# Layer 0 of a two-layer graph network with experts: aggregating normalized tokens and multiplying by the weights afterwards

## The chip, the cores and the metric

The kernel runs on one core of a Trainium2 chip. The metric is the device time of one execution in microseconds (us); several executions are measured and the median counts. The engines are TensorE (PE, with its weight loads shown apart as PEld), VectorE (DVE), ScalarE (ACT), GpSimd (POOL) and SyncE (SP), which here only issues DMAs.

## The reference

3327 tokens of 256 features go through two layers. Each layer is a graph aggregation followed by a mixture of 8 experts of which every token uses 2. Cut to what matters here (layer 0; layer 1 has another aggregation and other experts and isn't touched):

```python
def _L0_gnn_ref(x, adj, W, b):
    support = jnp.matmul(x, W)              # 256x256 weights
    out = jnp.matmul(adj, support) + b      # adj: 3327x3327
    return jax.nn.relu(out)

x = x + _L0_gnn_ref(_layernorm(x), adj, L0_gnn_W, L0_gnn_b)
x = x + _L0_ffn_ref(_layernorm(x)[None], Wg, bg, W1, b1, W2, b2)[0]   # top 2 of 8 experts
x = x + _L1_gnn_ref(_layernorm(x), adj, ...)
x = x + _L1_ffn_ref(_layernorm(x)[None], ...)[0]
```

So layer 0 computes adj · (LN(x) · W) + b. All of it is in float32.

## The kernel before, in words

**Tiles.** The tokens are padded to 3328, which is 26 tiles of 128 (`NT`). `x` [128, 26, 256] holds the tokens and stays in SBUF, and `s` of the same shape holds what the aggregation reads. The transposed adjacency matrix is read in 13 panels of 256 output tokens (`PW`, `NPAN`). A panel is two pieces of 13 tiles each (`NCHUNK`, `CJ`), 1664 KB a piece. Six pieces fit into a ring of buffers (`ring`, `RING`), which is three panels; `load_panel` (L335) loads them on SP's queue.

**Feature stage (L1022 to L1039).** For groups of 2, 2, 4, 4, 6 and 8 tiles DVE computes mean and 1/deviation (`statistics`, L258). PE turns each tile of `x` with transposes (`turned_tiles`, L304), ACT copies the result to SBUF (L305), PE multiplies it by `proj_sb` (`node_features`, L312), and ACT scales it by 1/deviation into `s` (L317). The mean is taken out of the weights once, with two matmuls (L1030) and one subtraction on DVE (L1033). So PE has 52 transposes and 52 products of [128x128] by [128x256] here, and the trace shows each float32 product as two instructions.

**Aggregation (`aggregate`, L344).** For each panel PE takes the pieces as weights and `s` as the moving operand, 52 products (L358), and gets the sums token by token in two PSUM tiles `ps_g`. DVE adds bias, ReLU and `x` (`add_relu`, L322, L323). ACT counts for each panel how many elements of the adjacency matrix are positive (`count`, L1046: 8 `sign` instructions a piece), which layer 1 needs.

**After a panel (`after0`, L1056).** DVE normalizes the panel's tokens (`layernorm`), multiplies them by the gate's weights (`scores`, L378, 16 instructions), takes the two best experts (`top_two`, `rt_both` L415) and their softmax (`weights`; the exponential is on ACT, L443). A panel later `list_tokens` (L457) ranks the tokens of each expert with small matmuls on PE (`pr`, L464 and L465), and POOL scatters the rows to the experts' lists in DRAM (`scatter`, L482). The engines work in the order in which the program's scheduler put the instructions, and each engine's queue is in order.

**Zeros of the lists (`fill`, L1003).** The first 256 rows of each expert's list, of both layers, are set to zeros with a spare row number in column `ID` (the last of 258). For each of the 16 lists POOL sets a [128, 2 x 258] tile (L1009, L1010) from a pool of two, and SP writes it to DRAM in rows of 1032 bytes (L1013). This is in `after0` of panels 0 and 1. `after0` of panel 0 also turns the two gates' weights by two DMAs from DRAM to DRAM of 2048 elements of 4 bytes each (L1062), and POOL loads the first to all partitions (`load_gate`, L247).

**After the panels.** The experts' blocks start at L865 on PE. Their first two steps don't need the last panel's tokens.

**DMA on SP.** SP's DMAs share eight completion semaphores in turn, so a DMA is issued only when the eighth before it has landed.

Of the kernel before, what the change touches and what calls it, by code (L numbers as in the profile page):

```python
# [22 lines left out]
P = 128  # L23
# [53 lines left out]

BEGUN, FIRST_TILES, MORE_TILES = 12, 14, 22
WARM = 32
# [11 lines left out]
def gnn_moe_two_layers(  # L91
# [39 lines left out]

    proj_sb = const.tile([P, DC, D], F32, name="proj_sb")
    for t, n in [(0, 2)] + [(t, 4) for t in range(2, NT, 4)]:
        nc.sync.dma_start(out=x[:, t : t + n, :], in_=x_in[:, t : t + n, :])
        if t == 0:
            nc.sync.dma_start(out=proj_sb, in_=g0_w.rearrange("(c p) n -> p c n", p=P))
# [10 lines left out]
    mean = ring[RING - 1][:, 0:P]  # L147
    nc.gpsimd.memset(mean, 1.0 / D)
# [95 lines left out]
    gates = []  # L244

# [62 lines left out]
    def node_features(i, lhsT, w_sb, scale=None):  # L308
# [6 lines left out]
        if scale is None:  # L315
            return nc.scalar.copy(s[:, i, :], ps)
        return nc.scalar.activation(s[:, i, :], ps, AF.Copy, scale=scale)  # L317
# [12 lines left out]
    def piece(pan, k):  # L330
        return ring[(pan * NCHUNK + k) % RING].rearrange("p (c w) -> p c w", w=PW)

    last_piece, output_loads = [], []

    def load_panel(pan, prepare, earlier=()):  # L335

        for k in range(NCHUNK):
            a = piece(pan, k)
            with behind(earlier):
                d = nc.sync.dma_start(out=a, in_=adjT[pan, k])  # L340
            last_piece[:] = [d]
            prepare(pan, k, a)

    def aggregate(b_sb, prepare, after, loaded=0, count=None):  # L344

        for pan in range(NPAN):
# [4 lines left out]
            if count:  # L351
                count(pan, chunks)
# [14 lines left out]
            after(pan)  # L367

# [634 lines left out]
    def fill(xlist):  # L1003

        with tc.issue_after(last_feature.ins):
            for e in range(E):
                zeros = blk.tile([P, H // P, SB], F32, name="wide").rearrange("p h b -> p (h b)")
                zeros = zeros[:, 0 : SG * RW].rearrange("p (g d) -> p g d", g=SG)
                nc.gpsimd.memset(zeros, 0.0)  # L1009
                nc.gpsimd.tensor_scalar(  # L1010
                    zeros[:, :, ID], slot, float(AWAY + SPARE + (LATE + e) * SB), None, ALU.add
                )
                nc.sync.dma_start(  # L1013
                    out=xlist[e * NP : e * NP + SB, :].rearrange("(g p) d -> p g d", p=P),
                    in_=zeros,
                )

    deviation = {}
    for t0, n0 in [(0, 2), (2, 2), (4, 4), (8, 4), (12, 6), (18, 8)]:  # L1022
        _, rs = statistics(t0, n0)
        deviation.update((t0 + g, rs[:, g : g + 1]) for g in range(n0))
        for t in range(t0, t0 + n0, 2):
            xT = turned_tiles([x[:, t + g, :] for g in range(2)])
            if t == 0:
                ps = psy.tile([P, D], F32, name="ps_mean", tag="py")
                for c in range(DC):
                    nc.tensor.matmul(  # L1030
                        ps, lhsT=mean, rhs=proj_sb[:, c, :], start=(c == 0), stop=(c == DC - 1)
                    )
                nc.vector.tensor_tensor(  # L1033
                    proj_sb, proj_sb, ps.unsqueeze(1).to_broadcast([P, DC, D]), ALU.subtract
                )
            for g in range(2):
                last_feature = node_features(
                    t + g, xT[:, :, ts(g, P)], proj_sb, deviation[t + g]
                )  # L1039

    def count(pan, chunks):
        with tc.issue_after(last_feature.ins):
# [451 lines left out]
```

## Time and profile before

| | |
|---|---|
| median of 3 executions | 1244.86 us (1243.46 to 1245.89) |
| the profiled execution | 1245.38 us, its span 1243.6 us, 1.8 us around it |
| PE busy | 1202.0 us, 97% of the span |
| first aggregation matmul of layer 0 | starts at 44.30 us |
| last aggregation matmul of layer 0 | ends just before 344.87 us |
| layer 0's panels, first to last | 300.6 us for 13 |

The span runs from the first instruction to the last. A row of a timeline has its start and its duration in us, the engine ("SPq" is SP's queue), the line, the instruction and the tiles as out<-in. A row of waits names who waited for whom: total us, times, longest. A row by stage has for each engine the busy time and the instructions, then PEclk (the granted TensorE clock as a share of full speed), the DMA engines' busy share and GB/s.

### The profile page before, as it was taken

Reading aid. Unit: us, or ns where it says so; the run is one execution under the profiler, and the core shown is the slowest. Engines: PE = TensorE matmul, PEld = TensorE weight load, DVE = VectorE, ACT = ScalarE, POOL = GpSimd, SP = SyncE. Lnnn points to the kernel's source line nnn. Section 1 sums busy time; section 2 is a strip of 40 time slices with the busy share of each in tenths; the row PEclk is TensorE's granted clock in tenths of the full one; section 3 lists DMA queues with packets and bytes.
Section 4 is the critical chain, followed back from the end, with each engine's and each line's share of the span. In section 5 each row is a group of like instructions: output and inputs, shape, how many; then the busy total and the mean of one; then the engine's idle time right before and its main releaser. Section 6 shows DMA issues by size and latency. Waiting matters only on the chain. (4 is left out here: it accounts for less than half of the span.)

```text
span 1243.6 us, 18251 instructions
## 1 busy us (share of the span) xinstructions
PE 1202.0 (97%) x5853; PEld 1040.3 (84%) x5853; DVE 698.0 (56%) x2812; ACT 522.5 (42%) x963; POOL 280.9 (23%) x367
## 2 busy tenths in 40 slices
PE   7999899999999999999999999999999999999993
PEld 6888788888888888888888888888888888877882
DVE  5064967768755111211111166658999998875464
ACT  4785654551022222222232235895555453043331
POOL 2022313112122111111111110002422323254441
PEclk9999899999999999999999999999999999999997
DMA  9568445544266567575757676344554442476697
GB/s 346 169 194 279 158 169 200 179 146 155 98 215 208 181 197 237 178 230 180 232 173 242 209 273 237 110 149 152 192 182 167 166 176 85 122 247 206 200 296 236
DMA packets 119738, 241.60 MB, mean 194 GB/s; under 512 B 21568, under 2 KB 90192, under 8 KB 112592
## 3 DMA queue, kind: packets, MB, share of 16 engines
q1 hardware_dynamic: 107984, 208.23, 50.2%
q0 software_dynamic: 11104, 31.59, 7.0%
q8 instruction: 48, 0.79, 0.3%
q14 instruction: 58, 0.48, 0.1%
q10 hardware_dynamic: 544, 0.52, 0.1%
HBM read 203.99 MB, written 36.33 MB: 193 GB/s over the span
## 5 line engine op out<-in xcount | busy, mean ns | idle before, releaser
L358 PE MATMUL ps_g<-s,ring 128*128 128x256 f32 x2704 | 591.0, 381 | 0.0
L358 PEld LDWEIGHTS ps_g<-s,ring 128*128 128x128 f32 x2704 | 514.2, 191 | 69.2
L865 PE MATMUL ps_h<-xT,ring 128*128 128x256 f32 (+1 forms) x1176 | 250.1, 366 | 2.7 <-DVE xT L856 1.1
L865 PEld LDWEIGHTS ps_h<-xT,ring 128*128 128x128 f32 x1176 | 205.5, 191 | 39.2 <-ACT wide L872 4.8
L872 ACT ACTIVATE wide<-ps_h,ring 128x256 f32<-128x256 f32 (+1 forms) x240 | 110.2, 459 | 286.0 <-PE ps_h L865 285.0
L378 DVE SCALAR_TENSOR_TENSOR rt_product<-xn,gate 128x256 f32<-128x256 f32 x400 | 197.0, 493 | 12.4
L904 PE MATMUL ps_y<-ring,wide 128*128 128x256 f32 x896 | 200.4, 379 | 0.0
L482 POOL DMA_INDIRECT xlist<-xn,rt_idx x104 | 106.3, 1023 | 371.6 <-DVE ln_ve L269 296.0
L904 PEld LDWEIGHTS ps_y<-ring,wide 128*128 128x128 f32 x896 | 167.2, 190 | 20.9
L1046 ACT ACTIVATE sign<-ring,below 128x416 bf16<-128x416 f32 x208 | 133.5, 642 | 71.6 <-DMA ring<-in_adjT 65.5
L482 POOL DMA_INDIRECT ys<-narrow,index x56 | 54.3, 969 | 331.9 <-DVE narrow L912 245.9
L1197 ACT ACTIVATE ring<-ring 128x3328 f32<-128x3328 f32 x22 | 65.4, 2979 | 87.2 <-DVE ring L1196 56.6
L856 DVE COPY xT<-ptb 128x512 f32<-128x512 f32 (+1 forms) x29 | 19.0, 654 | 146.3 <-PE ptb L853 146.3
L911 DVE TENSOR_TENSOR narrow<-ps_y,ring 128x256 f32<-128x256 f32 x56 | 23.8, 424 | 133.7 <-PE ps_y L904 132.2
L322 DVE TENSOR_TENSOR gnn_t<-ps_g,gnn_b_sb 128x256 f32<-128x256 f32 x52 | 21.9, 421 | 119.4 <-PE ps_g L358 106.4
L482 POOL DMA_INDIRECT ys<-wide,index x58 | 57.8, 996 | 61.2 <-DVE wide L912 35.3
L1198 ACT ACTIVATE ring<-ring 128x3328 f32<-128x3328 f32 x22 | 65.4, 2979 | 0.6
L872 ACT ACTIVATE narrow<-ps_h,ring 128x256 f32<-128x256 f32 (+1 forms) x64 | 28.9, 453 | 68.6 <-PE ps_h L865 66.5
L443 ACT ACTIVATE rt_d<-rt_d 128x2 f32<-128x2 f32 x26 | 5.3, 202 | 123.2 <-DVE rt_d L442 123.2
L904 PE MATMUL ps_y<-s,narrow 128*128 128x256 f32 (+1 forms) x200 | 49.0, 386 | 0.1
L266 DVE BATCH_NORM_STATS2 ln_st<-x 128x6 f32<-128x256 f32 x104 | 42.9, 419 | 6.1 <-DMA x<-in_x 5.0
L1196 DVE TENSOR_SCALAR ring<-ring 128x3328 f32<-128x3328 f32 x22 | 41.3, 1882 | 0.0
(212 smaller groups left out, 983.9 us busy)
## 6 DMA issues: line engine op xcount, KB each, us to landing
ring<-in_adjT SPq DMA_DIRECT2D x52, 1664.0 KB, 7.3
ring<-in_f_w1T SPq DMA_DIRECT2D x30, 1024.0 KB, 6.1
ring<-in_f_w2T SPq DMA_DIRECT2D x30, 1024.0 KB, 7.8
ring<-xlist SPq DMA_DIRECT2D x52, 258.0 KB, 3.0
ring<-in_f_w SPq DMA_DIRECT2D x36, 256.0 KB, 3.6
ring<-ys SPq DMA_DIRECT2D x14, 512.0 KB, 5.2
ring<-in_f_b SPq DMA_DIRECT2D x34, 128.0 KB, 8.0
xlist<-wide SPq DMA_DIRECT2D x16, 258.0 KB, 6.4
```

The costliest lines, as they stand in the source:

```text
L266: nc.vector.bn_stats(out=st, in_=x[:, t0 + g, :])
L358: nc.tensor.matmul(ps[it], lhsT=chunks[k][:, c, ts(it, P)], rhs=s[:, j, :], start=(j == 0), stop=(j == NT - 1),)
L378: nc.vector.scalar_tensor_tensor(product, xn[:, g, 0, 0:D], 1.0, gate[:, e, :], ALU.mult, ALU.mult, accum_out=sc[:, g, e : e + 1],)
L482: d = nc.gpsimd.indirect_dma_start(out=a[:, :], out_offset=bass.IndirectOffsetOnAxis(ap=index, axis=0), in_=rows_, in_offset=None,)
L865: nc.tensor.matmul(ps, lhsT=w1[:, c, ts(hc, P)], rhs=xT[:, c, :], start=(c == 0), stop=(c == DC - 1),)
L872: nc.scalar.activation(hT[:, hc, :], ps, func, bias=bb1[:, hc : hc + 1])
L904: last_product[:] = [nc.tensor.matmul(ps, lhsT=hT[:, hc, ts(g, P)], rhs=w2[:, hc, :], start=(hc == 0), stop=(hc == hc_n - 1),)]
L911: nc.vector.tensor_tensor(y[:, g, :], ps, bb2, ALU.add)
L1046: nc.scalar.activation(sign, a[:, :, ts(i, GROUP)], AF.Sign, bias=below, accum_out=positive[:, pan, i, k : k + 1],)
L1196: nc.vector.tensor_scalar(a, a, 0.0, None, ALU.max)
L1197: nc.scalar.activation(a, a, AF.Square)
L1198: nc.scalar.activation(a, a, AF.Tanh)
```

## The change

1. The feature stage is gone. DVE normalizes each tile straight into `s` (`layernorm(..., xn=s[...])`, one instruction a tile more), with the same groups and the same statistics.
2. The aggregation is `aggregate_first`. `s` gives the weights and the panel's piece is the moving operand, so the sums come out turned: two PSUM tiles [128 features x 256 tokens]. The number of products is the same, 52 a panel. ACT copies the two sums to SBUF (`g`), and PE multiplies them by `proj_sb`, 4 products a panel (`finish`), 6 tiles (`BEHIND` = 5) into the next panel, or at once after the last one. `add_relu` and `after0` of the panel follow `finish`.
3. Panels 0 and 1 go side by side over the first 13 tiles, then each does its second 13.
4. The loads at the start are in another order: x tiles 0 and 1, then the same tiles of the first pieces of panels 0 and 1, and so on for (2, 2), (4, 4) and (8, 5); then x's tiles 13 to 25 in one; the first gate's turn; `proj_sb`; the second pieces of panels 0 and 1; the second gate's turn; panel 2; the zeros of both lists; panel 3 and on.
5. The zeros of both lists come from one tile that POOL sets once. For each of the 16 lists there are now two DMAs: 257 zeros a row (1028 bytes), and a second one that writes 256 single elements of 4 bytes, the row numbers. All 32 stand on SP's queue behind panel 2 and ahead of panel 3.
6. The warming matmuls at the start are 54 in place of 32.

In the scheduled order of the changed program, ACT copies the sums of panel 2 behind 13 of the 16 counts of panel 3, those of panel 3 behind 14 of the 16 of panel 5, and those of panels 4 to 9 behind the first 6 counts of the panel three further on, the last five of these behind the exponential (L443's) of the panel before. PE's ranking matmuls of panel p stand just behind `finish` of panel p + 1. From the first expert block on, PE's order is the same as before.

```diff
-WARM = 32
+BEHIND = 5
+WARM = 54
...
+    def piece(pan, k):
+        return ring[(pan * NCHUNK + k) % RING].rearrange("p (c w) -> p c w", w=PW)
+
+    def turn_gate(w):
+        g = dram.tile([E, D], F32, name=f"gate{len(gates)}")
+        with nc.allow_non_contiguous_dma("a few thousand elements"):
+            d = nc.sync.dma_start(out=g.rearrange("e d -> d e"), in_=w)
+        gates.append(g)
+        return d
-    for t, n in [(0, 2)] + [(t, 4) for t in range(2, NT, 4)]:
+    for t, n in [(0, 2), (2, 2), (4, 4), (8, CJ - 8), (CJ, NT - CJ)]:
         nc.sync.dma_start(out=x[:, t : t + n, :], in_=x_in[:, t : t + n, :])
-        if t == 0:
-            nc.sync.dma_start(out=proj_sb, in_=g0_w.rearrange("(c p) n -> p c n", p=P))
+        if t < CJ:
+            for pan in range(2):
+                nc.sync.dma_start(
+                    out=piece(pan, 0)[:, t : t + n, :], in_=adjT[pan, 0, :, t : t + n, :]
+                )
+    turn_gate(f0_wgT)
+    nc.sync.dma_start(out=proj_sb, in_=g0_w.rearrange("(c p) n -> p c n", p=P))
...
+    def aggregate_first(b_sb, w_sb, begin, count, after):
+        sums, waiting = {}, []
+        def start(pan):
+            sums[pan] = [psy.tile([P, PW], F32, name="ps_g", tag="py") for _ in range(DC)]
+        def add(pan, j):
+            for c in range(DC):
+                nc.tensor.matmul(
+                    sums[pan][c],
+                    lhsT=s[:, j, ts(c, P)],
+                    rhs=piece(pan, j // CJ)[:, j % CJ, :],
+                    start=(j == 0),
+                    stop=(j == NT - 1),
+                )
+        def finish():
+            pan, g = waiting.pop()
+            for it in range(PW // P):
+                ps = psh.tile([P, D], F32, name="ps_o", tag="ph")
+                for c in range(DC):
+                    nc.tensor.matmul(
+                        ps, lhsT=g[:, c, ts(it, P)], rhs=w_sb[:, c, :], start=(c == 0),
+                        stop=(c == DC - 1),
+                    )
+                add_relu(x[:, pan * (PW // P) + it, :], ps, b_sb)
+            after(pan)
+        def rest(pan, first):
+            for j in range(first, NT):
+                add(pan, j)
+                if waiting and j == first + BEHIND:
+                    finish()
+            g = work.tile([P, DC, PW], F32, name="xnT", bufs=2)
+            for c in range(DC):
+                nc.scalar.copy(g[:, c, :], sums[pan][c])
+            waiting.append((pan, g))
+        loaded = RING // NCHUNK
+        for pan in range(loaded):
+            load_panel(pan, lambda pan, k, a: None, begun=1 if pan < 2 else 0)
+            if pan == 1:
+                turn_gate(f1_rT)
+        begin()
+        for pan in range(2):
+            start(pan)
+        for j in range(CJ):
+            for pan in range(2):
+                add(pan, j)
+        for pan in range(NPAN):
+            if pan > 1:
+                start(pan)
+            if loaded < min(pan + RING // NCHUNK, NPAN):
+                load_panel(loaded, lambda pan, k, a: None)
+                loaded += 1
+            count(pan)
+            rest(pan, CJ if pan < 2 else 0)
+        finish()
...
-    def fill(xlist):
-        with tc.issue_after(last_feature.ins):
-            for e in range(E):
-                zeros = blk.tile([P, H // P, SB], F32, name="wide").rearrange("p h b -> p (h b)")
-                zeros = zeros[:, 0 : SG * RW].rearrange("p (g d) -> p g d", g=SG)
-                nc.gpsimd.memset(zeros, 0.0)
...
+    def fill(*lists):
+        with tc.issue_after(last_piece[0].ins):
+            wide = blk.tile([P, H // P, SB], F32, name="wide").rearrange("p h b -> p (h b)")
+            zeros = wide[:, 0 : SG * ID].rearrange("p (g d) -> p g d", g=SG)
+            nc.gpsimd.memset(zeros, 0.0)
...
+            for xlist in lists:
+                for e in range(E):
+                    first = xlist[e * NP : e * NP + SB, :].rearrange("(g p) d -> p g d", p=P)
+                    nc.sync.dma_start(out=first[:, :, 0:ID], in_=zeros)
+                    with nc.allow_non_contiguous_dma("two elements of a partition"):
+                        nc.sync.dma_start(
+                            out=first[:, :, ID : ID + 1], in_=rows_f[:, e, :].unsqueeze(2)
+                        )
+    for t0, n0 in [(0, 2), (2, 2), (4, 4), (8, 4), (12, 6), (18, 8)]:
+        layernorm(t0, n0, xn=s[:, t0 : t0 + n0, :].unsqueeze(2))
...
     def after0(pan):
         if pan == 0:
-            with tc.issue_after(last_piece[0].ins):
-                for name, w in (("gate0", f0_wgT), ("gate1", f1_rT)):
...
             load_gate(gates[0])
-            fill(xlist0)
-        if pan == 1:
-            fill(xlist1)
...
-    aggregate(gnn_b_sb, lambda pan, k, a: None, after0, count=count)
+    aggregate_first(gnn_b_sb, proj_sb, lambda: fill(xlist0, xlist1), count, after0)
```

## The prediction

> **What bounds the kernel now.** The page comes first: PE is busy 97% of the span, and its largest group is the aggregation of both layers.
>
> ```profile
> PE 1202.0 (97%) x5853; PEld 1040.3 (84%) x5853; DVE 698.0 (56%) x2812; ACT 522.5 (42%) x963; POOL 280.9 (23%) x367
> L358 PE MATMUL ps_g<-s,ring 128*128 128x256 f32 x2704 | 591.0, 381 | 0.0
> ```
>
> So time is won where PE works less or waits less. PE's timeline from 0 to 46 us shows the stage that the change takes away:
>
> ```profile
> 1.06 3.37 PE L144 MATMUL ps_warm<-ones_sq 128*128 128x128 bf16 x32 [1.06 <-POOL ones_sq L140]
> 4.53 1.10 PE L1030 MATMUL ps_mean<-proj_sb,ring 128*128 128x256 f32 x4
> ...
> 8.11 0.66 PE L304 MATMUL pt<-ident,x 128*128 128x128 f32 x4 [2.04 <-DMA x<-in_x]
> ...
> 16.34 5.41 PE L312 MATMUL ps_s<-proj_sb,xnT 128*128 128x256 f32 x16 [3.25 <-ACT xnT L305]
> ...
> 26.48 1.04 PE L304 MATMUL pt<-ident,x 128*128 128x128 f32 x8
> 27.80 3.72 PE L312 MATMUL ps_s<-proj_sb,xnT 128*128 128x256 f32 x16 [0.29 <-ACT xnT L305]
> ...
> 44.30 1.89 PE L358 MATMUL ps_g<-s,ring 128*128 128x256 f32 x8
> ```
>
> From 21 us on it is bound by PE: 1.04 + 3.72 us for four tiles. The waits between 44 and 346 us, and then the stages by 5 us, show the one place where the panels lose time:
>
> ```profile
> ACT sign L1046 <- DMA ring<-in_adjT: 65.5, 15, 6.6
> POOL wide L1009 <- DMA xlist<-wide: 42.8, 12, 13.9
> DVE xn L445 <- ACT rt_d L443: 21.0, 12, 17.2
> ```
>
> ```profile
> 135.00:140.00 5.00, 1.66 (x8) 1.38 (x9) 4.35 (x23) 0.91 (x4) 0.00 (x0) 0.72 0.88 314
> 140.00:145.00 5.00, 5.00 (x16) 4.06 (x15) 4.55 (x23) 4.80 (x13) 1.56 (x2) 0.60 0.13 51
> ```
>
> Panel 3's pieces come late behind the zeros, ACT's counts wait for them, the exponential waits behind the counts, DVE waits 17.2 us for it, and PE then waits 3.72 us for `rt_both` (134.6 to 138.3). After that the granted clock is 0.72 and 0.60 for five microseconds each: 5 x 0.28 + 5 x 0.40 = 3.4 us more.
>
> **Layer 0's sum before.** A panel is 104 instructions; from 89.29 to 111.82 us that is 22.5 us, 0.216 us each. 44.3 + 13 x 22.5 + 3.7 + 3.4 + 1.0 (the ranking matmuls, the remainder) = 344.9 us, where the last panel does end.
>
> **The change, part by part.**
>
> *Feature stage, removed.* All of the 44.3 us go, and with them 52 transposes, the two mean matmuls, 13 + 26 copies on ACT and DVE's subtraction (0.69 us). The 52 products aren't removed: they become 13 x 4 in `finish`, 8 instructions a panel, 8 x 0.216 = 1.73 us, together 22.5 us.
>
> *First matmul.* x's first tiles let DVE start at 3.76 us. Its chain is at the third round at 6.06 us; after two statistics of the next pair (0.42 us each), four steps of 0.2 us and one normalization (0.37 us, half of L288's 0.73 for two) tile 0 is ready at 8.2 us, if x's tiles 2 and 3 have come by 6.6 us. They stand behind 0.75 MB, as those did that landed at 8.08 us; with that landing it is 10 us. I take 8.5. The 22 more warming matmuls (3.37 / 32 = 0.105 us each, 2.3 us) end near 6.7 us, before it.
>
> *First half of panels 0 and 1.* It is 104 instructions, 22.5 us, 1.73 us for a tile of both. DVE before the change had 26 statistics and six chains in 24.8 - 3.8 - 5.0 (waits for x) = 16.0 us; with twelve normalizations (4.4 us) tile 12 is ready at 24.2 us without a wait for x and at 29.2 with all of the former ones; PE wants it at 8.5 + 12 x 1.73 = 29.3. But the normalizations stand behind each group's chain (11 steps of 0.2 us), which no longer lies under the next group's statistics: that makes PE wait 0 to 5 us, and I take 2.5.
>
> *Panels after it.* 12 x 22.5 us as before, so the aggregation stays at 292.5 us in all.
>
> *Ranking of panel 0.* It stands behind `finish` of panel 1, 13.5 us after panel 0's `finish`, since panel 1 is only half. DVE from a panel's second sum (66.94) to `rt_both` (81.10) takes 14.2 us. PE waits 0.5 to 1.5; I take 1.
>
> *Copies on ACT.* Two of 0.47 us (row L317, the same shape) a panel, hidden in general: the exponential comes 15.2 us (66.94 to 82.16) after the last `finish`, five counts of 0.77 us and the copies end some 20.5 us after it, and PE comes back after 24.3. The piece that these counts need landed 6.8 to 8.0 us after its issue in the steady panels; it is issued at the panel's middle, 13.0 us in, and the exponential comes at 22.3, so it is there. After the last panel nothing covers the copies: 1 us.
>
> *The stall at 134 us* goes in this form: the zeros are earlier, POOL has no memsets between its scatters (42.8 us of waits, which no one else pays for), and the first gate is loaded earlier. What is late next is panel 3, below.
>
> *The zeros*, the open price. POOL's part is early and small. On SP's queue 32 DMAs now stand in one row between panel 2 and panel 3. Before, the queue was dense until 40 us and nearly empty afterwards, while the gates' elements went (SP's timeline, then the stages by 10 us):
>
> ```profile
> 18.54 23.69 SPq L1062 DMA_DIRECT2D gate<-in_f_rT  x1
> ```
>
> ```profile
> 30.00:40.00 10.00, 9.42 (x51) 8.00 (x50) 0.00 (x0) 6.16 (x13) 0.00 (x0) 1.00 1.01 395
> 40.00:50.00 10.00, 9.27 (x46) 7.95 (x45) 0.00 (x0) 7.39 (x19) 0.79 (x1) 1.00 0.16 12
> ```
>
> The second gate landed 42.3 us after its issue, at 60.9: 2 x 2048 elements of 4 bytes in 20.9 us, beside other transfers. Each is the shape of what the row numbers now are, and these are 16 x 256 = 4096 too. So they cost 0 to 21 us; I take 10, since their rows lie apart and their source is SBUF. The zeros: 258 KB at the 270 GB/s of 94 to 96 us is 0.96 us, 15 us for 16; two issued alone at 66.3 took 4.4 us, which would be 35. Up to panel 2 the queue holds the same 13.9 MB as up to 40 us, then the first gate's load (1 MB, 2.5 us) and the two gates (2 to 20, I take 8). Sum: 40 + 2.5 + 8 + 15 + 10 = 75.5; bounds 59 to 118. Panel 3's two pieces need some 10.5 us more: 86 (70 to 128).
>
> Who waits: panel 2 begins at 8.5 + 22.5 + 2.5 + 11.3 + 11.3 + 1.7 + 0.5 = 58.3 and panel 3 near 83.3. But ACT copies panel 2's sums behind 13 counts of panel 3, so its second piece has to be there by 82. It is 4 us late, PE waits that long, and the clock may drop as after 134.6: 1.7 us taken (0 to 3.4). Queued behind the copies are the counts and the next exponential, and DVE behind that, with 8 us of slack a panel.
>
> One rule speaks against this part. The Trainium skill, "DMA: Bandwidth & Descriptors", says in Specifications that transfers below 512 bytes are read, modified and written, and in "Rules for kernel authors" that a strided last dimension becomes one descriptor per element, so it should be made contiguous. No row here shows what such a write costs from SBUF; by the rule the row numbers would sit at the gates' end, 21 us, PE would wait 11 us longer, and the sum below would come to 1245.
>
> **Sum.** 8.5 + 292.5 + 22.5 + 1.0 + 2.5 + 1 + 1 + 4 + 1.7 = 334.7 in place of 344.9: 10.2 us less. From the experts on PE's order is the same, and their first two steps don't need the last panel, so the rest moves as a whole. 1245.4 - 10.2 = 1235.2; the median of the runs is 0.5 below that execution, so 1234.7. About 0.2% (2.5 us) is what a measurement of this kernel can tell from no change.
>
> **Rivals.**
>
> *The zeros are hidden.* If the elements go at the rate of the queue, panel 3's pieces are there by 82 and neither the 4 nor the 1.7 us are paid: 1229. For it: the gates' DMA share was only 0.16. Against it: the queue was no faster for that. Without the first half's wait it is 1226.5.
>
> *The zeros stop panel 3 (slower).* The place is SP's queue between panel 2 and 3. Each microsecond past 82 costs one; from 82 + 10.2 + 4 + 1.7, so when the second piece comes after 98 us instead of 86, the change loses. With the gates' price for the elements and 2.2 us for each list's zeros (35 us) it lands near 117, 19 us past that point: 1264, and more at the bound of 128. For it: both are rows of this trace. Against it: a dense queue moved zeros at 270 GB/s.
>
> *A starved start.* The second piece of panel 0 is wanted at 33.5 us; 8.8 MB stand before its end, of which 4.8 came by 18 us, and the rest at 395 GB/s takes 10 us: 28, and with 1 to 10 us of the gate 29 to 38. Then DMA and not DVE bounds the first half, 0 to 4.5 us: up to 1239.
>
> **How the numbers follow.** The forecast with a panel 3 late by up to 10 us, or a starved start: 1230.5 to 1242.4, chance 0.52. Hidden: 1226 to 1230.5, 0.28. No difference (1242.4 to 1247.4): 0.07. Slower, by the zeros: 0.13, up to 1265. So faster 0.80, same 0.07, slower 0.13. The range leaves out the upper tenth and little below: 1226.5 to 1248.
>
> **What would show it.** Right: the first matmul of the aggregation between 8 and 10 us; waits for `s` of a few us before 33; no wait for `rt_both` near 134; a wait for `xnT` or the ring near 85 us with a lower clock after it; panel pitch 24.3 us; layer 0's end near 335. Wrong: small elements that fill the queue past 100 us; ACT's copies late in every panel, so a pitch above 24.5; matmuls that take more than 0.216 us with `s` as the weights; or a last part that doesn't move with the end of layer 0.

## The result, and the profile after

| | kernel before | changed kernel |
|---|---|---|
| median beside each other, 9 executions each | 1242.85 us (1238.32 to 1247.17) | 1251.53 us (1248.83 to 1253.13) |
| profiled execution, its span | 1245.38 us, 1243.6 us | 1252.14 us, 1250.3 us |
| end of layer 0 (profile) | 345.6 us | 346.8 us |
| from there to the end of the span | 898.0 us | 903.5 us |

The changed kernel is slower: ratio 1.0079, 95% interval 1.0063 to 1.0095. The forecast was 1234.7. "End of layer 0" is here and below the end of the last panel's ranking matmuls and of the four transposes behind them (0.6 us), which belong to the first expert block.

The page of the changed kernel shows less work on PE, and a smaller share of it:

```profile
PE 1199.4 (96%) x5819; PEld 1036.6 (83%) x5819; DVE 707.3 (57%) x2837; ACT 509.4 (41%) x950; POOL 278.5 (22%) x337
```

PE's timeline at the start and at panel 3 (start and duration in us, what was idle before in brackets):

```profile
1.07 5.44 PE L163 MATMUL ps_warm<-ones_sq 128*128 128x128 bf16 x54 [1.07 <-POOL ones_sq L159]
10.53 9.68 PE L388 MATMUL ps_g<-ring,s 128*128 128x256 f32 x31 [4.01 <-DVE s L303]
...
92.66 5.45 PE L388 MATMUL ps_g<-ring,s 128*128 128x256 f32 x24 [3.50 <-DMA ring<-in_adjT]
102.94 1.65 PE L401 MATMUL ps_o<-proj_sb,xnT 128*128 128x256 f32 x3 [4.84 <-ACT xnT L415]
```

The feature stage is gone and the aggregation begins at 10.5 us instead of 44.3. But PE was idle for 4.0 us just before, and at panel 3 it waits twice, 8.3 us in all. PE's five largest waits up to 350 us (total, times, longest), after the change:

```profile
PE ps_g L388 <- DVE s L303: 5.6, 2, 4.0
PE ps_o L401 <- ACT xnT L415: 4.8, 1, 4.8
PE ps_g L388 <- DMA ring<-in_adjT: 4.1, 2, 3.5
PE ps_h L935 <- DVE xT L926: 2.1, 1, 2.1
PE pr L534 <- DVE rt_both L485: 1.7, 1, 1.7
```

In the table by stage the granted clock (the third number from the end) is half after both of the longer idle times (the row at 100 us mixes whole and half), and it is whole near 137 us, where the kernel before had its stall. Two rows show the DMA engines busy and moving little, at 44 us right behind the second gate's elements and at 62 us while the zeros go:

```profile
10.00:15.00 5.00, 4.47 (x11) 3.58 (x12) 4.69 (x25) 0.00 (x0) 0.00 (x0) 0.50 1.03 400
...
44.00:50.00 6.00, 6.00 (x29) 5.28 (x28) 0.00 (x0) 5.74 (x17) 0.00 (x0) 1.00 0.88 53
...
62.00:68.00 6.00, 6.00 (x30) 5.28 (x29) 5.58 (x26) 5.80 (x17) 0.61 (x1) 1.00 0.96 167
...
100.00:105.00 5.00, 2.06 (x5) 1.70 (x6) 0.23 (x2) 4.84 (x15) 0.00 (x0) 0.64 1.02 428
...
135.00:140.00 5.00, 5.00 (x25) 4.41 (x24) 4.54 (x18) 4.81 (x14) 3.98 (x5) 1.00 0.42 111
```

SP's queue says when: the issue of `proj_sb`, behind the first gate's turn, takes 12.9 us, and that of panel 2's first piece, behind the second gate's, 17 us. Panel 3 is issued at 80.6, behind the last of the zeros:

```profile
11.87 12.93 SPq L155 DMA_DIRECT2D proj_sb<-in_g_w  x1
...
26.43 17.03 SPq L350 DMA_DIRECT2D ring<-in_adjT  x1
...
79.63 0.50 SPq L1095 DMA_DIRECT2D xlist<-wide  x1
80.59 8.96 SPq L350 DMA_DIRECT2D ring<-in_adjT  x6
```

And ACT's timeline says why PE waits a second time. ACT could not begin panel 3's counts before 92.7, and the copies of panel 2's sums stand behind 13 of them:

```profile
92.70 0.64 ACT L1106 ACTIVATE sign<-ring,below 128x416 bf16<-128x416 f32 x1 [19.12 <-DMA ring<-in_adjT]
...
102.54 0.62 ACT L415 COPY xnT<-ps_g 128x256 f32<-128x256 f32 x2
```

### The profile page after: what moved, and what is told of

It is laid out like the page before. It is cut to its first block, busy times and chain, and to the rows that moved or that the text cites. A ratio compares the mean times of both kernels' runs of the same rounds, so it can differ in the third digit from the quotient of the medians.

```text
span 1250.3 us, 18161 instructions
## 1 busy us (share of the span) xinstructions
PE 1199.4 (96%) x5819; PEld 1036.6 (83%) x5819; DVE 707.3 (57%) x2837; ACT 509.4 (41%) x950; POOL 278.5 (22%) x337
## 4 chain that ended last, share of the span: by engine, by line
PE 87%; DMA 7%; SPq 3%; ACT 2%; issue 1%; DVE 1%; ACTq 0%; DVEq 0%
PE ps_g L366 23%; PE ps_h L935 19%; PE ps_y L974 19%; PE ps_g L388 18%; DMA xlist<-wide 3%; PE ptb L923 2%; PE ps_s L327 2%; PE ps_o L401 2%; PE ps_p L1215 1%; SPq L350 1%; DMA ring<-ys 1%; SPq L155 1%; DMA ring<-in_adjT 1%; ACT sign L1106 1%; DMA x<-in_x 1%
## 5 line engine op out<-in xcount | busy, mean ns | idle before, releaser
L388 PE MATMUL ps_g<-ring,s 128*128 128x256 f32 x1352 | 299.5, 383 | 9.8 <-DVE s L303 5.6
L388 PEld LDWEIGHTS ps_g<-ring,s 128*128 128x128 f32 x1352 | 258.1, 192 | 46.3 <-DVE s L303 6.2
L366 PE MATMUL ps_g<-s,ring 128*128 128x256 f32 x1352 | 294.2, 380 | 0.0
L366 PEld LDWEIGHTS ps_g<-s,ring 128*128 128x128 f32 x1352 | 256.0, 190 | 34.4
L448 DVE SCALAR_TENSOR_TENSOR rt_product<-xn,gate 128x256 f32<-128x256 f32 x400 | 199.7, 499 | 12.3
L926 DVE COPY xT<-ptb 128x512 f32<-128x512 f32 (+1 forms) x29 | 18.9, 653 | 147.3 <-PE ptb L923 147.3
L335 DVE TENSOR_TENSOR gnn_t<-ps_o,gnn_b_sb 128x256 f32<-128x256 f32 x26 | 11.0, 424 | 76.4 <-PE ps_o L401 76.4
```

Source lines behind the costliest of these rows:

```text
L366: nc.tensor.matmul(ps[it], lhsT=chunks[k][:, c, ts(it, P)], rhs=s[:, j, :], start=(j == 0), stop=(j == NT - 1),)
L388: nc.tensor.matmul(sums[pan][c], lhsT=s[:, j, ts(c, P)], rhs=piece(pan, j // CJ)[:, j % CJ, :], start=(j == 0), stop=(j == NT - 1),)
L448: nc.vector.scalar_tensor_tensor(product, xn[:, g, 0, 0:D], 1.0, gate[:, e, :], ALU.mult, ALU.mult, accum_out=sc[:, g, e : e + 1],)
```

## The experiments

Each kernel was timed against the kernel before on the same chip. The chips differ by up to 7 us (the kernel before had medians of 1242.85 here and of 1248 to 1250 in the experiments), so ratios are compared, and in the profiles the end of layer 0. The program's scheduler orders ACT's work anew for every kernel. The changed kernel's order (panel 2's copies behind 13 of panel 3's counts) stands in `after_again`, `warm92` and `behind10`, and `x_first` is close to it. In `zeros_late`, `zeros_back`, `list1_end`, `all_late`, `best` and `best2` these copies stand behind all 16 of panel 3's counts and 11 to 15 of panel 4's, so these runs change more than their edit says.

### Where the zeros stand: two kernels, and the zeros alone

`zeros_late` moves both lists' zeros, in their new form:

```diff
-    aggregate_first(gnn_b_sb, proj_sb, lambda: fill(xlist0, xlist1), count, after0)
+    aggregate_first(gnn_b_sb, proj_sb, lambda: None, count, after0)
     def after0(pan):
         if pan == 0:
             load_gate(gates[0])
+            fill(xlist0)
+        if pan == 1:
+            fill(xlist1)
```

> The changed kernel with one thing moved: the zeros keep their new form (257 zeros a row and the row numbers as single elements), but list 0's stand behind panel 3's pieces and list 1's behind panel 4's on SP's queue, where after0 of panels 0 and 1 puts them. Theory Z (the 32 DMAs ahead of panel 3 make it late): PE's waits of 3.5 and 4.8 us near 89 and 98 us and the half clock after them (3.4 us more) all go, 11.7 us in all, so the last panel ends near 334.5 and the time is 1240 (1238 to 1243). Rival G (the panel is late because the gates' single elements hold the queue before it, 26 to 50 us): panel 3's pieces still land after 85 us and the time stays at 1251 (1249 to 1253). Rival M (the stall only moves): panel 4 or 5 or the first ranking is late instead, with a half clock of its own, 1245 to 1249.

Measured: 1.0037 (1.0018 to 1.0056). Panel 3 is no longer late, and layer 0 ends at 343.1. But PE's timeline shows a wait for the copies one panel later:

```profile
94.90 1.99 PE L401 MATMUL ps_o<-proj_sb,xnT 128*128 128x256 f32 x8 [0.81 <-ACT xnT L415]
...
124.41 2.03 PE L401 MATMUL ps_o<-proj_sb,xnT 128*128 128x256 f32 x4 [4.88 <-ACT xnT L415]
```

ACT's timeline has the cause, the first piece of panel 5, which stands behind list 1's zeros:

```profile
109.56 0.64 ACT L1106 ACTIVATE sign<-ring,below 128x416 bf16<-128x416 f32 x1 [12.28 <-DMA ring<-in_adjT]
```

So theory Z holds for panel 3, G falls as the whole cause, and M holds for the rest: the zeros make a later panel late instead, and the copies of panel 3's sums stand behind counts of it.

`zeros_back` has the former `fill` (one DMA of 258 columns, the tiles from POOL) at the former place, in the changed kernel.

> The changed kernel with the zeros as before the change: one DMA of 258 columns for each of the 16 lists from POOL's pairs of tiles, put in by after0 of panels 0 and 1; the order of the loads, the aggregation and the warming matmuls stay changed. Theory Z: panel 3's pieces go first, 1240 as in the run with the zeros moved; what differs between the two is the form alone. If the old form brings back the former stall (exponential behind counts, a wait for rt_both of 3.7 us and a half clock), 1247. Rival G: 1251, as the changed kernel.

Measured: 1.0079 (1.0063 to 1.0095), as the changed kernel. PE's timeline has one longer wait in place of the two:

```profile
128.56 3.78 PE L401 MATMUL ps_o<-proj_sb,xnT 128*128 128x256 f32 x8 [8.53 <-ACT xnT L415]
```

The former place, nearly harmless before, now stops PE, because PE's products need copies that ACT makes behind counts of a late panel: ACT waits 13.5 us for the first piece of panel 6, which SP issues at 116.1, behind list 1's zeros. The expected 1240 was missed for that reason, not for the one given in the expectation (`rt_both`).

`zeros_only` has the new `fill` in the kernel before, called at panel 0's counts.

> The kernel before with only the zeros changed: the new form, both lists from one tile, all 32 DMAs between panel 2 and panel 3 on SP's queue; the gates' turns come behind them. Theory Z: the 32 DMAs take about 30 us of the queue, as in the changed kernel; they start near 40 us instead of 44, so panel 3's pieces, which also have the gates' 20 us ahead of them, land at 100 to 110 us where panel 3 is wanted at 112: the former stall at 134 us goes or moves by little, 1238 to 1246. Rival (the zeros cost only because of where they meet the faster start): 1237 to 1240, a gain of the stall's 7 us. Slower than 1247 would say that the elements cost the queue far more than 30 us.

Measured: 1.0104 (1.0081 to 1.0127), beyond both ranges. The expectation would have put a result above 1247 down to the elements, but the rows of zeros moved in 27 us by the DMA records, and the waits from 40 to 110 us name another cause:

```profile
DVE rt_product L378 <- DMA gate<-gate: 23.0, 1, 23.0
...
PE pr L464 <- DVE rt_sel L417: 14.9, 1, 14.9
```

Here the gates' turns stand behind the zeros, the first gate comes late, panel 0 isn't scored, and PE waits 14.9 us for its ranking, with 17 us of half clock from 90 us on. This run doesn't price the zeros; it shows what else stands in that queue.

### The start: `warm92` and `x_first`

```diff
-WARM = 54
+WARM = 92
```

> The changed kernel with 92 warming matmuls instead of 54 (0.1007 us each, 3.8 us more, so they end near 10.3 us where x's tiles arrive). Theory C (PE's 4.0 us of idle time before the first aggregation matmul at 10.5 us is what halves the clock until 16.1 us): the clock stays whole from the first aggregation matmul on, 3.4 us less up to 16 us, the last panel's end and the time 3.4 us earlier, 1248. Rival (PE then only waits for DVE's normalized tiles, which come at their own rate): the first half has 3.4 us more of waits for s and the time stays at 1251.

Measured: 1.0059 (1.0041 to 1.0076). The matmuls ended at 9.1 us and not at 10.3, since the later ones run at full clock (35 in the 3.4 us until 6.8, then 40 in 2.3 us), and PE was idle for 2.3 us instead of 4.0. The clock stayed whole through the first half. Layer 0's end came at 345.0, 1.4 to 1.9 us below the two profiles of the changed kernel, so theory C is right in kind and half of it was lost again: the first half then waited 2.8 us for `s` at 32.8 us, and panel 3 was late all the same.

`x_first` has this order, and 76 warming matmuls:

```diff
-x(0,2) a0 a1(0,2) x(2,2) a0 a1(2,2) x(4,4) a0 a1(4,4) x(8,5) a0 a1(8,5) x(13,13)
+x(0,2) x(2,2) a0 a1(0,2) x(4,4) a0 a1(2,2) x(8,5) a0 a1(4,4) x(13,5) a0 a1(8,5) x(18,8)
```

> The changed kernel with x's tiles one step ahead of the pieces at the start: x (0,2), x (2,2), then both panels' (0,2), x (4,4), both (2,2), and so on, x's tiles 13 to 17 ahead of the last part of the first pieces; and 76 warming matmuls. Theory C (the start loses 2 us to x's tiles 2 and 3, 3.4 us to the half clock behind the idle PE, and 1 to 1.6 us to the late tiles 13 to 25): first aggregation matmul at 8.0 to 9.0 us instead of 10.5 to 10.9, no half clock before 16 us, no wait for s near 34 us: 5 to 7 us less at 60 us. What comes after stays as it is, since panel 3 is late by SP's queue and not by PE: then part of it is lost again in a longer wait at panel 3, so 2 to 6 us are won in all, ratio 1.0035 to 1.0065.

Measured: 1.0049 (1.0031 to 1.0067). The first aggregation matmul came at 8.85 us, with no half clock behind it. But much of the lead was lost at once, for the second pieces of panels 0 and 1 (PE's waits, total, times, longest):

```profile
PE ps_g L391 <- DMA ring<-in_adjT: 6.0, 2, 5.2
```

They stand on SP behind the first gate's turn and `proj_sb`, and no earlier start of PE brings them sooner. The clock was half from 37.2 to 44.0 after the longer of these waits, and layer 0 ended at 342.4.

### The same two kernels again

`before_again` and `after_again` are the two kernels unchanged.

> The kernel before, unchanged, profiled a second time on the chip of the runs beside it. It is to tell whether the last 110 us of the span (layer 1's last blocks, which lasted 5.2 us longer in the changed kernel's profile and 8 to 10 us longer in the four first experiments) follow the chip or the change. Theory P (they follow the chip): its part from the first expert product (346.7 us) to the end is as long as in the changed kernel beside it, to within 2 us. Theory T (the change lengthens them): it stays 5 us or more shorter.

> The changed kernel, unchanged, profiled a second time and timed. Theory P: layer 0's last panel ends 1 to 3 us later than in the kernel before beside it, and the time is 1.002 to 1.005 of it, less than the 1.0079 seen first. Theory T: 1.007 to 1.009 again, with layer 0's end 1 to 3 us late and 5 us or more lost behind 1095 us.

`after_again` measured 1.0084 (1.0066 to 1.0103) and ends layer 0 at 346.4, as at first. `before_again` ends it at 340.3, 5.3 us sooner than in its first profile: there is no wait for `rt_both` and no half clock. From the end of layer 0 to the end of the span it takes 907.0 us, `after_again` 910.2. So the changed kernel does lose, and 6.1 us of it in layer 0. The last part differs by 3.2 us here, where the first two profiles had 5.5 (898.0 and 903.5); in all the profiles of the experiments it lies between 907 and 911. Neither theory holds alone; `before_third` and `best2` below settle more of it.

### Half of the zeros away: `list1_end`

```diff
-    aggregate_first(gnn_b_sb, proj_sb, lambda: fill(xlist0, xlist1), count, after0)
+    aggregate_first(gnn_b_sb, proj_sb, lambda: fill(xlist0), count, after0)
     def after0(pan):
+        if pan == 10:
+            fill(xlist1)
```

> The changed kernel with list 1's zeros (16 of the 32 DMAs) moved from between panels 2 and 3 to behind the last panel's pieces; list 0's stay. The 32 DMAs took about 30 us of the queue, so half of them gives panel 3's pieces back some 15 us: they land near 78 us, before panel 3 is wanted at 82. Theory Z: the waits of 3.5 and 4.8 us and the half clock after them go, 11.7 us less: 0.9% below the changed kernel beside it, and layer 0's end near 335. Rival G (the gates' elements hold the queue): the waits stay, and less than 2 us is won.

Measured: 1.0058 (1.0039 to 1.0077), layer 0's end 344.2. Panel 3 was issued at 69.5 instead of 80.6, and PE no longer waits for its piece. It waits for the copies instead:

```profile
101.08 2.54 PE L401 MATMUL ps_o<-proj_sb,xnT 128*128 128x256 f32 x5 [5.40 <-ACT xnT L415]
```

ACT's timeline, at panel 3's piece and at the copies:

```profile
78.63 0.64 ACT L1106 ACTIVATE sign<-ring,below 128x416 bf16<-128x416 f32 x1 [7.28 <-DMA ring<-in_adjT]
...
100.68 0.35 ACT L415 COPY xnT<-ps_g 128x256 f32<-128x256 f32 x1
```

ACT waited for panel 3's piece until 78.6, and from there it had 27 counts, two exponentials and a wait of 1.4 us for DVE in front of the copy at 100.7, 22 us in all; PE wanted the copy at 95.7. 11 of these counts are panel 4's, which in the changed kernel stand behind the copy. So there are two conditions for panel 3's piece: PE wanted it at about 84 (panel 2's start at 59.8 and a panel of 24.3), but ACT, in this run's order, by 78.6 - 5.4 = 73.2. With the changed kernel's order (9 counts of 0.77 us, an exponential for which DVE was ready there at 87.8, 4 more counts) the copy would have come near 91 by an estimate, in time. What half of the zeros cost with ACT's order kept, this run doesn't show.

### Distance or engine: `behind10` and `copies_dve`

```diff
-BEHIND = 5
+BEHIND = 10
```

> The changed kernel with finish 10 tiles behind instead of 5 (4.3 us later in the next panel). Theory Q (the products wait because ACT copies the sums behind counts that wait for a late piece; PE needs the copies only when finish comes): the waits for xnT (2.3 and 1.1 us in the last profile of the changed kernel, 4.8 in the first) and for rt_both near 70 us (1.65) go, the wait for panel 3's first piece (3.6) stays: 5 us or more less, layer 0's end 340 to 342, a ratio to the kernel before of 1.003 to 1.005 beside 1.0084. Rival (the copies are late by whole panels, whatever the distance): the waits for xnT shrink by no more than 1 us, ratio 1.007 to 1.009.

Measured: 1.0046 (1.0033 to 1.0060), the ratio as expected; layer 0's end in the profile, 344.4, is later than expected. PE's waits:

```profile
PE pr L534 <- DVE rt_both L485: 3.9, 2, 2.3
...
PE ps_o L401 <- ACT xnT L415: 1.8, 3, 1.1
```

The waits for the copies shrink to 1.8 us, and the one for panel 3's first piece is 1.4 here. The wait for `rt_both` near 70 us stays at 1.64, against the expectation: both of its `finish` calls moved together, so the distance between them is the same. A new one of 2.3 us comes at the last panel, whose predecessor's `finish` is now nearer to the end.

```diff
-                nc.scalar.copy(g[:, c, :], sums[pan][c])
+                nc.vector.tensor_copy(g[:, c, :], sums[pan][c])
```

> The changed kernel with the copies of the sums on DVE instead of ACT, so they no longer stand behind ACT's counts. Theory Q: the waits for xnT (2.3 to 4.8 and 1.1 us) go, ratio 1.004 to 1.006. Rival (DVE is late itself, since it waits for the exponential, which stands behind the same counts): PE's waits stay or move to ps_o and rt_both, ratio 1.007 to 1.012.

Measured: 1.0036 (1.0021 to 1.0050), layer 0's end 342.6. Of PE's waits the one for the piece stays, and the one for the copies is 1.6 us:

```profile
PE ps_g L388 <- DMA ring<-in_adjT: 3.8, 1, 3.8
...
PE ps_o L401 <- DVE xnT L415: 1.6, 1, 1.6
```

Two edits that touch neither DMA nor the zeros win 0.3 to 0.5% over the changed kernel's 1.0079 and 1.0084. So theory Q holds: the order of copies and counts on ACT turns a late piece into a wait of PE.

### All repairs together: `all_late`, `best`, `best2`

`all_late` has list 0's zeros behind panel 3, list 1's and the second gate's turn behind the last panel (at panel 10's `after0`), and 106 warming matmuls.

> The changed kernel with list 0's zeros behind panel 3's pieces, list 1's zeros and the second gate's turn behind the last panel's, and 106 warming matmuls. Theories Z and C together: no wait at panel 3 (3.5 + 4.8 and 3.4 of half clock), no half clock before 16 us (3.4), no second gate ahead of panel 2, at most 1 us of wait at panel 4: layer 0's end near 331 us, 15 us below the changed kernel, so a time of 0.990 to 0.994 of the kernel before. Rival M (stalls move to the next panel): layer 0's end near 341, a ratio of 0.998 to 1.002.

Measured: 1.0044 (1.0030 to 1.0058), layer 0's end 339.8 where 331 was expected. The first matmul still came at 11.2, with a half clock to 15.6; there were 1.6 us at 34, 1.65 for `rt_both`, and one wait of 2.1 us for the copies at 290, which halved the clock for one window. The net work (the length less the waits and less the clock's loss) was 318.9 us, not 316. The profiled execution took 1250.6 us, 2.5 less than the run's median, so this profile doesn't hold all that most executions lose.

`best` adds to that:

```diff
-BEHIND = 5
+BEHIND = 10
-WARM = 106
+WARM = 76
 # x's tiles ahead as in x_first
-    turn_gate(f0_wgT)
     nc.sync.dma_start(out=proj_sb, in_=g0_w.rearrange("(c p) n -> p c n", p=P))
...
             load_panel(pan, lambda pan, k, a: None, begun=1 if pan < 2 else 0)
+            if pan == 1:
+                turn_gate(f0_wgT)
```

> All the repairs together: x's tiles ahead, 76 warming matmuls, finish 10 tiles behind, proj_sb and the second pieces ahead of the first gate's turn, list 0's zeros behind panel 3's pieces, list 1's zeros and the second gate's turn behind the last panel. The net work of PE in layer 0 was 318.5 us at full clock in all profiles of the changed kernel. With the first matmul at 8.5 us and up to 3 us of waits that makes a layer 0 end of 327 to 330 us, against 340.3 in the undisturbed kernel before: 10 to 13 us less, of which 2 go at the first expert products, so a ratio of 0.991 to 0.994. If the ratio is 0.998 or more, a stall has moved to another panel or the part behind layer 0 has lost what was won.

Measured: 0.9965 (0.9952 to 0.9978), faster than the kernel before, but short of the expected 0.991 to 0.994. First matmul at 8.1, layer 0's end 334.1. The largest of the waits that are left for PE:

```profile
PE pr L536 <- DVE rt_both L487: 3.9, 2, 2.3
PE ps_g L390 <- DVE s L305: 1.9, 1, 1.9
```

`best2` changes three distances in `rest`:

```diff
-                if waiting and j == first + BEHIND:
+                if waiting and j == first + {1: 4, 2: 12, NPAN - 1: 5}.get(pan, BEHIND):
```

> The repaired kernel (ratio 0.9965) with three distances changed: finish of panel 0 comes 4 tiles into the rest of panel 1 instead of 10, that of panel 1 comes 12 tiles into panel 2, and that of panel 11 comes 5 tiles into panel 12. The two waits for rt_both (1.65 us near 70 and 2.3 us near 328) and the half clock behind the second (1.7 us) should go: 4 to 5.5 us less, layer 0's end near 329, ratio 0.992 to 0.994. If waits for rt_both stay at 1.6 us, the ranking is late by DVE's own chain and not by the distance, and the ratio is 0.996.

Measured: 0.9916 (0.9902 to 0.9929), layer 0's end 329.0. Both waits for `rt_both` are gone:

```profile
PE ps_g L390 <- DVE s L305: 2.1, 2, 1.3
PE ps_h L937 <- DVE xT L928: 2.1, 1, 2.1
...
PE ps_g L390 <- DMA ring<-in_adjT: 0.8, 1, 0.8
```

So the distance between two `finish` calls was the cause, and the changed kernel with its waits taken away is 0.8% faster than the kernel before as it stands. The kernel before got no such repairs: its own start has waits of 5.2 us for the copies and 2.0 us for x's tiles, and what they would give there was not tried.

### What the stall of the kernel before is worth: `before_third` and `before_list1`

> The kernel before, unchanged, profiled a third time. The first profile had the stall at 134 us (3.7 us of wait for rt_both and 3.4 us of half clock) and layer 0's last panel ended at 345.6; the second had no stall and ended at 340.3. Theory S (the stall is a matter of a few us of DMA time and most executions don't have it): no wait for rt_both, end at 340 to 341, and 906 to 908 us from the first expert product to the end. Rival (most executions have it): a wait of over 2 us and an end of 343 to 346.

Measured in the one execution: 1250.3 us, on a chip where the kernel before had a median of 1248.11. PE's timeline:

```profile
134.73 0.18 PE L464 MATMUL pr<-rt_both,before 128*128 128x8 bf16 x1 [3.30 <-DVE rt_both L415]
```

There is a wait of 3.3 us, yet layer 0 ends at 339.3, since the aggregation had begun at 41.1 (44.3 and 45.6 in the other two profiles) and the clock stayed whole. Neither theory foresaw that.

`before_list1` is the kernel before with the call of `fill(xlist1)` moved from panel 1 to panel 6, with PE's, ACT's and DVE's order unchanged. The issue of the zeros is also tied to the last piece of a panel in place of the feature stage (`issue_after`).

> The kernel before with only list 1's zeros moved from panel 1's end to panel 6's; the order on PE, ACT and DVE is the same. Panel 3's and 4's pieces then have half of the zeros ahead of them, so the stall at 134 us can't arise. The ratio to the kernel before says how much the stall is worth in the median: theory S (most executions don't have it): 0.999 to 1.001. Rival (most have it): 0.993 to 0.996.

Measured: 0.9998 (0.9981 to 1.0015), layer 0's end 339.5, no stall. So on that chip the stall costs the median execution 0.2 us, at most 2.4 by the interval, if the zeros cost nothing at panel 6, where the profile has no wait. In the two profiles of the unchanged kernel on other chips it doesn't show in the end: with the early start (41.1) the wait takes the lead back, with the late one (45.6) there is no wait. In the first profile a start at 44.3, the stall and its half clock came together.

## Why the prediction was wrong

The step that failed is panel 3: the sum has its pieces "4 us late, PE waits that long", and PE waited 8.3 us, with 2.65 us of half clock behind it. The start was mis-sized by nearly as much (4.8 us), and the base held a stall that the undisturbed kernel before doesn't have. Layer 0's sum, term by term, from the changed kernel's first profile; the net work is what is left of the length. The loss to the clock is half of PE's time at half clock, 10.5 to 16.1 us and 102.9 to 108.2 us.

| term | predicted | measured |
|---|---|---|
| first matmul | 8.5 | 10.5 |
| net work (292.5 + 22.5 + 1.0) | 316.0 | 318.6 |
| half clock at the start | none | 2.8 |
| first half's waits | 2.5 | 2.3 |
| ranking of panel 0 | 1 | 1.65 |
| last copies | 1 | in the net work |
| panel 3's waits | 4 | 8.3 |
| half clock after them | 1.7 | 2.65 |
| end of layer 0 | 334.7 | 346.8 |

**The kernel it was measured against.** The sum began at 344.9, which holds the stall at 134 us and its half clock. That was one execution. Two more profiles and `before_list1` end at 339.3 to 340.3. So some 5 to 6 of the 10.2 us forecast were no gain over those executions, which are of other chips; on the first chip there is one profile, 2.5 us above the later median of 9. The text had the median beside the profile, but the median is one number and doesn't tell whether the stall is in it. The price of the half clock was also read too high: its 3.4 us begin at 137.2, while PE stood until 138.3, which the wait of 3.7 counts already. PE worked at half clock from 138.3 to 144.0, which costs 2.8; the sum's remainder took up the difference.

**The first matmul.** This is 2.0 us, and the half clock behind it 2.8. The text named both values, 8.5 if x's tiles 2 and 3 come by 6.6 us and 10 if they come at 8.1, as such tiles did in the trace. They landed at 8.9. The row was there and the better end was taken. That the warming matmuls, ending at 6.5, would leave PE idle for 4 us, and what a halved clock then costs, was not priced at all, though the kernel before had the same thing behind 3.25 us at 13 us.

**Panel 3.** The place was right, SP's queue between panels 2 and 3. The sum had the queue done with the zeros at 75.5 and the pieces landed at 86. SP issued them at 80.6, but rows of zeros were still moving until 86.4, POOL's scatters beside them, and the pieces landed at 92.6 and about 97: 11 us later than forecast. By the DMA records two terms were too small. "40 + 2.5 + 8" has the zeros begin at 50.5, and their first row moved at 58.3; the zeros and elements then took 28 us and not 25. The pieces themselves took the 10.5 us of the sum. The first of these terms, which is the larger, holds the two gates' turns. In `all_late` the second gate's turn isn't there, and panel 2's last packet ends at 50.6 instead of 60.3. The row of `all_late` at 44 us moves eight times as much as the changed kernel's above:

```profile
44.00:50.00 6.00, 6.00 (x30) 5.28 (x29) 0.00 (x0) 5.76 (x16) 0.00 (x0) 1.00 1.02 435
```

So the turn of one gate cost the queue some 9.7 us, where the sum has 8 for both. Moving this turn alone was not tried.

The form of the wait was right as well: the text saw that the copies stand behind 13 counts and gave the piece a due time for ACT. The two waits of 3.5 and 4.8 us are that one lateness. ACT needs 10.3 us from the first piece to the copies, and without the first wait PE would have asked for them at 94.6 (89.2 and 5.4), so the piece was due at 84.3 and landed 8.3 us late. Without moving a DMA `behind10` leaves 1.9 us of it and `copies_dve` 5.4. PE itself came to panel 3 at 89.2 and not at 83.3, which kept the wait from being longer still.

The price of the elements, the open number of the forecast, was not what decided, as far as the records tell. They put the 32 DMAs at 24.6 us of all 16 engines, estimated 25; but 20.7 of that are the rows of zeros and only 3.9 the elements. Whether the elements slow the rows between them is open.

The sentence on the Trainium skill, "DMA: Bandwidth & Descriptors" (Rules for kernel authors), put the elements at the gates' 21 us. The page's rule of one descriptor per element agrees with the trace, which has 4096 records of 4 bytes for these 16 DMAs (4618 between 58 and 87 us with all others). But each took 14 ns, so 21 us was too dear.

**Net work.** 2.6 us more than taken. 0.6 of it are the four transposes, which the sum's end (344.9, and 334.7) doesn't hold, and the last copies' 1 us is in it too. In before's undisturbed profile the stretch takes 294.6 us with the transposes and 294.0 without, where the sum has 293.5. That leaves 24.0 us for `finish` with its surroundings, 1.85 a panel rather than 1.73. The exchange of weights and moving operand costs nothing that shows: in `best2`'s profile the new form and layer 1's unchanged one are

```profile
L390 PE MATMUL ps_g<-ring,s 128*128 128x256 f32 x1352 | 295.6, 380 | 2.9 <-DVE s L305 2.1 <-DMA ring<-in_adjT 0.8
L368 PE MATMUL ps_g<-s,ring 128*128 128x256 f32 x1352 | 294.2, 380 | 0.0
```

**"The rest moves as a whole."** Nearly right. The first expert product waits 2.1 us instead of 1.1, as the last copies and products stand before it. Otherwise the part behind layer 0 takes 909.2 us in `before_third`, 909.0 in `before_list1` and 908.9 in `best2`, all on one chip. The 5.5 us between the first two profiles there are 1.0 of this, 1.7 of a half clock near 1140 us that lasted two windows instead of one, and waits for lists and outputs in the last 50 us that differ in every profile; how much of the last is the change's is open, and by the runs on one chip it is little. One loss there is the changed kernel's own: in seven profiles of its variants (`zeros_late`, `zeros_back`, `warm92`, `x_first`, `list1_end`, `copies_dve`, `all_late`) the clock is half for one window behind that wait, 1.7 us more; in none of the kernel before is it. The forecast was 10.2 us less and the pair measured 8.7 us more, 18.9 apart: 11.5 are layer 0's sum without the transposes, 5 to 6 the base, and the last 1 to 2 lie behind layer 0 or between executions.

**What was right.** No wait for `rt_both` near 134 us, the first half's waits, the ranking of panel 0, the clock's fall after panel 3, and matmuls of the same length. The rival "The zeros stop panel 3" had the place and the sign, but for pieces later than 98 us; here about 97 was enough, with the start and the base against the forecast. "A starved start" was there as well: `x_first` shows it at 5.2 us.

## What to carry to other kernels

A stall in one profile is not yet a term of the median: profile the base again, or take away the stall's cause alone and time that, before a forecast counts on its end. When an engine in a chain takes over work for the critical engine, look at what stands ahead of that work in its queue and at the latest transfer that this waits for, since the critical engine inherits that wait. A change with a good idea can lose on distances: here the same products were 0.8% slower or 0.8% faster than the kernel before, by where 32 DMAs of zeros, two gate turns, x's tiles and four products a panel stood. And an edit that moves one thing can make the scheduler move others: compare the engines' orders before a run is read as one change.

## What the runs showed of the hardware

**The clock's windows.** All falls and rises of the granted clock lie on a grid of 3.413 us, the same through a whole execution, and what counts is the idle time inside one such window and not the gap. `all_late`, after one gap of 2.1 us (window, PE busy, granted clock before the DMA numbers):

```profile
288.64:292.05 3.41, 1.31 (x6) 0.86 (x5) 2.85 (x16) 0.74 (x3) 0.00 (x0) 1.00 1.04 385
292.05:295.46 3.41, 3.41 (x13) 2.57 (x12) 1.00 (x3) 0.00 (x0) 0.00 (x0) 0.50 0.55 175
```

`before_third`, where a gap of 3.3 us falls into two windows:

```profile
129.74:133.15 3.41, 1.69 (x8) 1.14 (x6) 3.13 (x16) 0.42 (x2) 0.00 (x0) 1.00 0.24 47
133.15:136.57 3.42, 1.84 (x12) 1.63 (x13) 2.91 (x16) 1.09 (x4) 0.00 (x0) 1.00 0.95 389
```

A window with PE busy for 1.31 us (38%) halves the clock in the next; two with 1.69 and 1.84 us (50 and 54%) don't. Over all 17 profiles, from 7 us on, every whole-clock window with PE busy for 40% or less was followed by a half clock, and none with more than 52%; between these both occur. The half clock lasts one window where PE is busy throughout it, and longer where it isn't: two windows with some 65% busy in the first (before's first profile, 137.2 to 140.6), three in `zeros_back`, where PE stood for 8.5 us. So a gap of 2 to 4 us is worth its own length and nothing, 1.7 or 2.6 to 2.8 us more, by where it falls.

The Trainium skill, "TensorE: Matmul & The Clock Gate" (What's actually happening), has the window of 3413 ns and that it runs freely, and the traces agree. Its advice in "Why this matters for your kernels" is to have no gaps above some 3 us; here 2.1 us was enough, and 3.3 us once was not, so the measurement decides.

**A row of zeros.** By the DMA records a row of 1028 bytes (the new form) took 73 to 81 ns on average in nine profiles, and 92 to 100 ns in `all_late`, `best` and `best2`; a row of 1032 bytes (the old form) 49 to 54 ns in five. For 4096 rows that is 18.7 to 20.8 us of 16 engines in the nine, with 3.9 us for the elements in the changed kernel's first profile, against 12.6 to 13.7. The medians are close, 47 to 58 ns against 47: the average is made by rows that took long. Whether the length, the elements between the rows or what else moves at that time does it was not tried.

**Small elements hold up what stands behind them.** The second gate's 2048 elements of 4 bytes take 9 to 10 ns each by the records, 1.3 us of 16 engines. But of panel 2's packets of 13312 bytes, those that start from 44 to 50 us, right behind them, took 2.7 to 3.8 us each on average, where they take 0.5 us otherwise.
